# Attention and top-1 LoRA: projection products, scalings and one turned tile rearranged where one sequence follows another

## The chip, the cores and the metric

The kernel runs on one core of one Trainium2 chip. The metric is the device time of one launch in microseconds, as the median of several runs. Engines are named as in the profile: PE is TensorE, DVE VectorE, ACT ScalarE, POOL GpSimd, SP SyncE (which issues all DMAs here).

## The reference

Four sequences of 1024 rows and 1024 columns, all in fp32, pass through a pre-LayerNorm causal attention of 32 heads (32 columns each, rotary positions) and then through a LayerNorm and a top-1 choice among 8 LoRA adapters of rank 16. Cut to what is computed:

```
B, S, D, H, E, R = 4, 1024, 1024, 32, 8, 16
n = layernorm(x)
q, k, v = rotary(n @ wq), rotary(n @ wk), n @ wv       # per head of 32 columns
p = softmax(causal(q @ k.T / sqrt(32)))
y = x + (p @ v) @ wo
m = layernorm(y)
e, gate = argmax(m @ route_w.T), max(m @ route_w.T)    # per row, one of 8
out = y + gate * ((m @ A[e].T) @ Bw[e].T)
```

## The kernel before, in words

**Units.** The work is cut into 32 units (b, g): sequence b (0 to 3) and group g (0 to 7) of four heads, run in this order. A unit takes some 80 to 87 us. Unit 7 is the last of the first sequence, 15 of the second, 23 of the third, 31 of the fourth.

**The frame of a unit.** `SLOTS` gives eleven slots. Nine are score rounds (`score_round`, L393: small matmuls into the one PSUM buffer `s`, copied by ACT at L417, the mask added on POOL at L420); two, "second" and "first", multiply probabilities by values (`apply`: `av` at L573, into the same PSUM buffer; the sums' reciprocals `rec` at L534, their spread `by` at L547 and L548, the product `at` at L593). Behind each round DVE finds the rows' maxima (`top` L438, `both` L459), ACT takes the exponentials of an earlier round (L467), and DVE turns probabilities in blocks of 32 (L492) for `av`. Each engine works through its instructions in the order in which they are issued; what is issued late is behind everything issued before it.

**What fills a unit.** Between rounds, `fill` and `do_some` take steps from the list `between[u]`, a share after every round, by each step's cost (1.0 for one product). This list is written by hand for the changes of sequence and woven for the others. It holds:
- the chains of unit u+1 (`chain`, L302): q, k and v for either half of the rows, each 8 products of 128x512 (L313) into one PSUM bank; then ACT copies the bank out, and for q and k DVE and POOL apply the rotary (L345 to L351);
- `project` (L679) of the sequence before, for the row tile t = g: 16 products `po` (L690), two banks of 8; each takes a 256 KB piece of wo from one of four `chunk` buffers, and the load of the piece four places on is issued behind it. The second bank's end issues the residual sum (L696) and the LayerNorm of y (`find_moments`, and L186 into `yn`);
- the `tail` of the tile before, t = g-1, in four steps: `turn` (eight PE transposes into two PSUM banks `pt_f`, L198, copied out by ACT at L200 and by DVE at L204), `route` (16 products `ph`, L711, and a chain of five short DVE instructions to `wh`, L730), `turn_hidden` (one transpose `pw`, L740) and `adapt` (two matmuls `pf`, L750, two sums on DVE, L753, and the store of `out_y`, L754).

**The norm of the next sequence.** Class `Norm` (L233) prepares x of sequence b+1 tile by tile: `load`; `find` (two BATCH_NORM_STATS2 at L175, L177, L179 on DVE, then 1/sqrt on POOL, L181, as `rstd_a`); `scale` (L186 on DVE, in place); `turn` (eight transposes `pt_a`, L198, and two copies by ACT, L200 and L202, into `xnT`), which scales first if that hasn't been done, and then loads the tile named in `after`. Five rows of x stand in the pool `row`; at the later changes tiles 3, 4 and 6 are loaded into the buffers of `qT` and `kT` (`homes`). For b = 1, `scale` also finds the next tile's moments.

**Three changes of sequence.** Around units 5 to 7 (first), 15 (second) and 23 (third), the steps are written out by hand: `behind(last_v, at, step)` puts a step of the norm behind a given product of the list of the unit before, `between[-2].insert` into the list of the one before that, and `change_steps` (L788) builds the last unit's list. At the first change nothing else is there. At the second and third this list starts with eight products held back from unit 15's or 23's own chain v, second half (`h`), the tail of tile 6, and the projection of tile 7 (`p`); then come the new sequence's chains, with the rest of `p` woven in.

**PSUM.** Four banks in turn (`ps`: chains, `po`, `pt_a`, `pt_f`, `ph`, `pw`, `pf`, `pr`) and the buffer of four banks for `s` and `av`. A bank is taken again when its copy or sum is done.

Of the kernel before, what the change touches and what calls it, by code (L numbers as in the profile page):

```python
# [71 lines left out]
def tile_preln_attn_then_top1_lora(  # L72
# [26 lines left out]
    NT = S // P  # L99
# [91 lines left out]
    def transposed(dst, src, name, scalar_only=False):  # L191

        pts = []
        for half in range(NC // 4):
            pt = bank([P, 4, P], f"pt_{name}_{half}")
            for i in range(4):
                c = 4 * half + i
                nc.tensor.transpose(pt[:, i, :], src[:, c * P : (c + 1) * P], eye_sb)  # L198
            pts.append(pt)
        nc.scalar.copy(dst[:, 0:4, :], pts[0])  # L200
        if scalar_only:
            nc.scalar.copy(dst[:, 4:8, :], pts[1])  # L202
        else:
            nc.vector.tensor_copy(dst[:, 4:8, :], pts[1])  # L204
# [28 lines left out]
    class Norm:  # L233
# [24 lines left out]
        def find(self, t):  # L258
            while self.found <= t and self.found in self.x:
                k = self.found  # L260
                self.moments[k] = find_moments(self.x[k], f"a{self.b}_{k}")
                self.found += 1
# [24 lines left out]
        def scaling(self, t):  # L287
            return Step(lambda: self.scale(t), 0.0)

        def turning(self, t):  # L290
            return Step(lambda: self.turn(t), 2.0 if self.b == 0 else 1.3)
# [364 lines left out]
    def finish_steps(b, t, kind="stream"):  # L656
# [6 lines left out]
        st = {}  # L663
        name = f"{b}_{t}"
# [35 lines left out]

        def turn():
            st["ynT"] = st["yn"].rearrange("p (c k) -> p c k", k=P)
            transposed(st["ynT"], st["yn"], f"f{name}", scalar_only=at_end)

        def route(ks=None):
            ph = bank([P, E + ER], f"ph_{name}")
# [53 lines left out]
        chains = []  # L760
# [27 lines left out]
    def change_steps(u, norm, project, tail, held):  # L788

        p, h, turning, scaling = project, held, norm.turning, norm.scaling
        out, chains = [], []
        for n, tb in (("q", 0), ("k", 0), ("q", 1), ("k", 1), ("v", 0), ("v", 1)):
            chains += chain(u, n, tb)
        if p:
            turn, route, turn_hidden, adapt = tail
            find = norm.finding
            out += [*h[:2], turn, *h[2:4], turning(2), h[4], find(3), route, h[5], scaling(3), find(4)]
            out += [h[6], turn_hidden, h[7], p[0], adapt, Step(lambda: norm.load(7), 0.0), scaling(4)]  # L800
            out += [p[1], find(5), p[2], scaling(5), turning(3), p[3], p[4], turning(4), *p[5:8]]
            chains = weave(chains[:-6], p[8:]) + chains[-6:]
            out += [*chains[:2], find(6), *chains[2:4], scaling(6), turning(5), *chains[4:6], find(7)]
            out += [*chains[6:8], scaling(7), turning(6), *chains[8:14], turning(7)]
            return out + chains[14:]
        out += [*chains[:3], scaling(5), turning(4), *chains[3:7], scaling(6), turning(5)]
        out += [*chains[7:12], scaling(7), turning(6), *chains[12:16], turning(7)]
        return out + chains[16:]

    USUAL = (("q", 0), ("k", 0), ("q", 1), ("k", 1), ("v", 0), ("v", 1))  # L810
# [2 lines left out]
    def behind(steps, at, step):  # L813

        steps.insert(steps.index(at) + 1, step)
# [4 lines left out]
    for u, (b, g) in enumerate(units):  # L820
        project, new_tail = [], []
        if b:
            fetch, (project,), new_tail = finish_steps(
                b - 1, g, "resident" if u == len(units) - 1 else "stream"
            )
            if g:
                apart = 3 if g + 1 == NG and u + 1 < len(units) else 8
                between[-1].insert(max(0, len(between[-1]) - apart), fetch)
            else:
                late_fetch[u] = fetch  # L830

        if u + 1 < len(units) and g + 1 == NG:
            last_v = between[-1]
            if b:
                norm = Norm(b + 1, {0: (2,), 2: (5,), 3: (6,)}, {3: "q", 4: "k", 6: "q"})
                load = [Step(lambda norm=norm, t=t: norm.load(t), 0.0) for t in range(2)]
                for at, step in (
                    (own["k", 0][0], load[0]),  # L840
                    (own["v", 0][0], norm.finding(0)),
                    (own["v", 0][1], load[1]),
                    (own["v", 0][2], norm.scaling(0)),
                    (own["v", 0][6], norm.turning(0)),
                    (own["v", 0][7], norm.finding(1)),
                    (own["k", 1][0], norm.scaling(1)),
                    (own["k", 1][3], norm.turning(1)),
                    (own["k", 1][5], norm.finding(2)),
                    (own["k", 1][7], norm.scaling(2)),
                ):  # L850
                    behind(last_v, at, step)
            else:
                norm = Norm(b + 1, {0: (5,), 1: (6,), 2: (7,)})
                for t, at in enumerate((("k", 1), ("k", 1), ("k", 1), ("v", 1))):
                    behind(last_v, own[at][(1 + 3 * t) % NC], norm.turning(t))
                behind(last_v, own["v", 1][5], norm.scaling(4))
                behind(last_v, own["k", 0][0], norm.scaling(3))
                behind(last_v, own["q", 0][6], norm.scaling(2))
                for t in (1, 0):
                    between[-2].insert(18 + 22 * t, norm.scaling(t))  # L860
                between[-2].insert(0, Step(lambda norm=norm: norm.load(*range(TB + 1)), 0.0))
            steps = change_steps(u + 1, norm, project, tail, held)
            norms[b + 1] = norm
        else:
            steps = []
            held = []
            if u + 1 < len(units):


                ends = g + 2 == NG and b + 1 < B  # L870
                own = {}
                for n, tb in ENDING if ends else USUAL:
                    own[n, tb] = chain(u + 1, n, tb)
                    if ends and b and (n, tb) == ("v", 1):
                        held = own[n, tb]
                    else:
                        steps += own[n, tb]
            if not steps:
                steps = list(project)
            elif b and not g:  # L880
                steps = steps[:36] + weave(steps[36:], project)
            else:
                steps = weave(steps[:-6], project) + steps[-6:]
            if u + 1 == len(units):
                new_tail6 = tail
            n = len(steps)
            for k, s in reversed(list(enumerate(tail))):
                steps.insert(6 + k * n // 7, s)
        between.append(steps)
        tail = new_tail  # L890
# [248 lines left out]
```

## Time and profile before

| | |
|---|---|
| median of 3 runs | 2777.18 us (2774.65 to 2780.03) |
| profiled execution: time, span, mean granted PE clock | 2774.93 us, 2773.1 us, 0.994 |
| PE busy | 2695.8 us, 97% |
| DVE, ACT, POOL busy | 77%, 63%, 23% |
| DMA over the span | 113 GB/s |
| PE idle or waiting, second change (1170 to 1242 us) | 15.3 us |
| PE idle or waiting, third change (1857 to 1930 us) | 13.3 us |

How to read it: the span runs from the first to the last instruction on the core. The times of groups are read from one profiled execution. In a timeline row there stand the start in us, the duration, engine, line, operation, what is written and read, tile sizes and the number of instructions; in brackets the idle time ahead and the instruction that ended it. `pt_a`, `pt_f`, `st_a` and so on are tiles' names with the numbers left out. The granted clock is a share of full speed. A share of busy time over the whole span is a mean over many stages; the waits of an engine and the rows around them say which of them count.

### The profile page before, as it was taken

What the parts mean: (1) busy time and instruction counts of PE and PEld (TensorE: products, weight loads), DVE (VectorE), ACT (ScalarE), POOL (GpSimd) and SP (SyncE); (2) the same over time, 40 slices, a digit from 0 to 9 for tenths busy, and PEclk for the clock granted to TensorE, in tenths of its full rate; (3) what the DMA queues carried; (4) which work ended last, traced back from release to release, by engine and by line L of the source; (5) the groups of instructions that cost most, each with busy time, mean ns of one, the idle gap of its engine ahead of it and who ended that gap; (6) DMA issues with size and microseconds to landing.
All of it is one profiled execution on the core that took longest, in us unless ns stands there. A gap on an engine that the chain in (4) does not pass through costs nothing.

```text
span 2773.1 us, 84079 instructions
## 1 busy us (share of the span) xinstructions
PE 2695.8 (97%) x35328; PEld 1328.7 (48%) x35328; DVE 2133.2 (77%) x4201; ACT 1754.4 (63%) x5030; POOL 637.7 (23%) x900
## 2 busy tenths in 40 slices
PE   8999999899999999989999999998999999999998
PEld 5444444444444544445444455444544444544445
DVE  4888889887777777777777777887777777777655
ACT  2877787776666666656666666765566666666421
POOL 2222222222222222222222222212222222222000
PEclk9999999999999999999999999999999999999999
DMA  3222231225454445551644444454255444436421
GB/s 116 51 55 55 58 102 47 75 55 161 127 138 123 117 120 149 154 146 49 174 143 123 135 115 124 135 163 136 66 158 149 130 133 125 118 117 194 127 67 54
DMA packets 448011, 317.86 MB, mean 115 GB/s; under 512 B 150288, under 2 KB 371728, under 8 KB 447632
## 3 DMA queue, kind: packets, MB, share of 16 engines
q1 hardware_dynamic: 447632, 312.47, 40.4%
q8 instruction: 278, 4.55, 0.7%
q14 instruction: 101, 0.83, 0.1%
HBM read 262.59 MB, written 49.81 MB: 113 GB/s over the span
## 4 chain that ended last, share of the span: by engine, by line
PE 81%; DVE 14%; ACT 2%; POOL 1%; issue 1%; DMA 0%; SPq 0%; POOLq 0%; ACTq 0%; DVEq 0%
PE po L690 15%; PE pq L313 14%; PE pk L313 13%; PE pv L313 12%; PE s L406 11%; PE av L573 9%; DVE top L438 4%; DVE pr L492 4%; PE pf L750 2%; PE ph L711 2%; DVE both L459 1%; PE pr L547 1%; PE pt_f L198 1%; ACT pr L417 1%; ACT pr L467 1%
## 5 line engine op out<-in xcount | busy, mean ns | idle before, releaser
L467 ACT ACTIVATE pr<-pr,both 128x256 f32<-128x256 f32 (+15 forms) x2048 | 1045.0, 519 | 47.9 <-DVE both L459 47.5
L438 DVE TENSOR_REDUCE top<-pr 128x2 f32<-128x960 f32 (+15 forms) x768 | 651.1, 894 | 252.1 <-POOL pr L420 251.5
L417 ACT COPY pr<-s 128x640 f32<-128x640 f32 (+14 forms) x544 | 525.2, 1016 | 500.7 <-PE s L406 500.1
L492 DVE STREAM_TRANSPOSE pr<-pr 128x1024 f32<-128x1024 f32 (+11 forms) x768 | 664.4, 907 | 34.3 <-ACT pr L467 31.0
L313 PE MATMUL pv<-xnT,wv 128*128 128x512 f32 x1024 | 488.1, 604 | 0.0
L420 POOL TENSOR_TENSOR pr<-pr,causal_sb 128x128 f32<-128x128 f32 x512 | 238.7, 473 | 1077.1 <-ACT pr L417 1068.3
L313 PE MATMUL pq<-xnT,wq 128*128 128x512 f32 x1008 | 478.6, 601 | 0.6 <-ACT xnT L200 0.6
L313 PE MATMUL pk<-xnT,wk 128*128 128x512 f32 x1008 | 477.0, 603 | 2.0 <-ACT xnT L200 2.0
L406 PE MATMUL s<-kT,qT 32*32 32x256 f32 (+4 forms) x17408 | 394.3, 386 | 10.0 <-ACT pr L417 5.8
L467 ACT ACTIVATION_READ_ACCUMULATOR pr<-pr,both 128x1 f32 x2048 | 400.8, 196 | 0.0
L690 PE MATMUL po<-chunk,attn 128*128 128x512 f32 x736 | 377.3, 598 | 0.3 <-DMA chunk<-in_wo 0.3
L406 PEld LDWEIGHTS s<-kT,qT 32*32 32x32 f32 x17408 | 187.9, 103 | 268.0 <-issue 103.4
L313 PEld LDWEIGHTS pk<-xnT,wk 128*128 128x128 f32 x1008 | 182.2, 190 | 238.8 <-issue 234.9
L313 PEld LDWEIGHTS pv<-xnT,wv 128*128 128x128 f32 x1024 | 187.3, 192 | 217.7 <-issue 213.4
L313 PEld LDWEIGHTS pq<-xnT,wq 128*128 128x128 f32 x1008 | 182.1, 191 | 224.9 <-issue 221.2
L573 PE MATMUL av<-pr,vals 64*32 64x256 f32 (+3 forms) x12288 | 272.2, 319 | 6.6 <-DVE pr L492 5.8
L573 PEld LDWEIGHTS av<-pr,vals 64*32 64x32 f32 x12288 | 213.4, 106 | 114.3 <-issue 43.2
L459 DVE TENSOR_TENSOR both<-top 32x4 f32<-32x4 f32 (+3 forms) x1152 | 215.1, 187 | 23.8
L690 PEld LDWEIGHTS po<-chunk,attn 128*128 128x128 f32 x736 | 136.1, 191 | 164.5 <-issue 152.5
L548 ACT COPY by<-pr 128x512 f32<-128x512 f32 x64 | 37.5, 586 | 254.8 <-PE pr L547 254.8
L593 DVE TENSOR_TENSOR at<-av,by 128x256 f32<-128x256 f32 x128 | 48.1, 418 | 164.8 <-ACT by L548 164.8
L690 PE MATMUL po<-wo,attn 128*128 128x512 f32 x256 | 117.5, 600 | 0.0
(87 smaller groups left out, 1718.5 us busy)
## 6 DMA issues: line engine op xcount, KB each, us to landing
chunk<-in_wo SPq DMA_DIRECT2D x368, 256.0 KB, 3.5
vals<-vd SPq DMA_DIRECT2D x256, 128.0 KB, 4.1
x<-in_x SPq DMA_DIRECT2D x58, 512.0 KB, 5.7
wq<-in_wq SPq DMA_DIRECT2D x32, 512.0 KB, 4.0
wk<-in_wk SPq DMA_DIRECT2D x32, 512.0 KB, 3.9
wv<-in_wv SPq DMA_DIRECT2D x32, 512.0 KB, 4.3
vd<-vT SPq DMA_DIRECT2D x128, 128.0 KB, 4.8
out_y<-x SPq DMA_DIRECT2D x32, 512.0 KB, 2.8
```

Source lines behind the costliest of these rows:

```text
L313: nc.tensor.matmul(at["p"], lhsT=wt[:, c, :], rhs=xnTs[b, tb][:, c, :], start=(c == 0), stop=(c == NC - 1),)
L406: nc.tensor.matmul(sc[i * SQ : (i + 1) * SQ, h, at : at + w].rearrange("p (j k) -> p j k", k=SQ), lhsT=of_q[rows, 2 * t + half], rhs=of_k[ ...
L417: nc.scalar.copy(pr[:, :, k0 : k0 + w], sc[:, :, at : at + w])
L420: nc.gpsimd.tensor_tensor(diagonal, diagonal, causal_sb.unsqueeze(1).to_broadcast([P, HG, SQ]), ALU.add)
L438: nc.vector.tensor_reduce(top[:, k, h : h + step], places[u, t][:, h : h + step, :], AX.X, ALU.max, negate=True,)
L459: nc.vector.tensor_tensor(dst[rows], src[rows], src[other], op)
L467: nc.scalar.activation(pr[:, h, :], pr[:, h, :], AF.Exp, bias=tops[u, t][:, h : h + 1], accum_out=dens[u, t // QT][:, t % QT, h : h + 1],)
L492: nc.vector.transpose(pr, pr)
L573: nc.tensor.matmul(avs[half][h * HD : (h + 1) * HD, t0:, :], lhsT=v[rows, j, h * HD : (h + 1) * HD], rhs=rhs, start=(j == 0), stop=(j == n ...
L690: nc.tensor.matmul(st["po"], lhsT=lhsT, rhs=rhs, start=(c == start), stop=(c == stop))
L711: nc.tensor.matmul(ph, lhsT=st["ynT"][:, c, :], rhs=w[:, c - i * RA, :], start=(c == 0), stop=(c == NC - 1),)
L750: nc.tensor.matmul(pf, lhsT=st["whT"], rhs=rhs, start=True, stop=True)
```

## The change

Three things, all in the order in which steps are issued or in the engine that copies:

1. `turn` of a tail copies the second half by ACT (L202) instead of DVE (L204) for tile 6 (`t == NT - 2`) too. This is tile 6 of the first, second and third sequences, which runs at the second and third change and in unit 31; the fourth's is so already.
2. In `change_steps`, with a projection there: twelve products of `p` come ahead of the new chains, where there were eight (two changes, so eight products in all), four of them before `turn_hidden`, where there were none; finds and scalings have new places among them, and the turnings of tiles 2 and 3 are one to a few steps later. Without a projection (first change): `scaling(5)` leaves this list, `scaling(6)` and `scaling(7)` stand further ahead of their turnings.
3. Ahead of it: at the second and third change the finds of tiles 1 and 2 and the scaling of tiles 1 and 2 get earlier places in the list of unit 14 or 22. At the first change the scalings of tiles 0 and 1 go to earlier places in unit 5, those of tiles 2 to 5 in unit 6.

```diff
@@ -700,7 +700,8 @@
 
         def turn():
             st["ynT"] = st["yn"].rearrange("p (c k) -> p c k", k=P)
-            transposed(st["ynT"], st["yn"], f"f{name}", scalar_only=at_end)
+
+            transposed(st["ynT"], st["yn"], f"f{name}", scalar_only=at_end or t == NT - 2)
 
         def route(ks=None):
             ph = bank([P, E + ER], f"ph_{name}")
@@ -796,15 +797,16 @@
         if p:
             turn, route, turn_hidden, adapt = tail
             find = norm.finding
-            out += [*h[:2], turn, *h[2:4], turning(2), h[4], find(3), route, h[5], scaling(3), find(4)]
-            out += [h[6], turn_hidden, h[7], p[0], adapt, Step(lambda: norm.load(7), 0.0), scaling(4)]
-            out += [p[1], find(5), p[2], scaling(5), turning(3), p[3], p[4], turning(4), *p[5:8]]
-            chains = weave(chains[:-6], p[8:]) + chains[-6:]
+            load_last = Step(lambda: norm.load(7), 0.0)
+            out += [*h[:2], turn, *h[2:4], find(3), p[0], h[4], turning(2), h[5], p[1], route, scaling(3)]
+            out += [find(4), h[6], p[2], h[7], p[3], turn_hidden, scaling(4), *p[4:6], adapt, load_last]
+            out += [p[6], find(5), p[7], turning(3), scaling(5), *p[8:10], turning(4), *p[10:12]]
+            chains = weave(chains[:-6], p[12:]) + chains[-6:]
             out += [*chains[:2], find(6), *chains[2:4], scaling(6), turning(5), *chains[4:6], find(7)]
             out += [*chains[6:8], scaling(7), turning(6), *chains[8:14], turning(7)]
             return out + chains[14:]
-        out += [*chains[:3], scaling(5), turning(4), *chains[3:7], scaling(6), turning(5)]
-        out += [*chains[7:12], scaling(7), turning(6), *chains[12:16], turning(7)]
+        out += [*chains[:2], turning(4), scaling(6), *chains[2:6], turning(5), scaling(7)]
+        out += [*chains[6:11], turning(6), *chains[11:16], turning(7)]
         return out + chains[16:]
 
     USUAL = (("q", 0), ("k", 0), ("q", 1), ("k", 1), ("v", 0), ("v", 1))
@@ -841,23 +843,25 @@
                     (own["v", 0][0], norm.finding(0)),
                     (own["v", 0][1], load[1]),
                     (own["v", 0][2], norm.scaling(0)),
+                    (own["v", 0][4], norm.finding(1)),
                     (own["v", 0][6], norm.turning(0)),
-                    (own["v", 0][7], norm.finding(1)),
-                    (own["k", 1][0], norm.scaling(1)),
+                    (own["v", 0][7], norm.scaling(1)),
+                    (own["k", 1][2], norm.finding(2)),
                     (own["k", 1][3], norm.turning(1)),
-                    (own["k", 1][5], norm.finding(2)),
-                    (own["k", 1][7], norm.scaling(2)),
+                    (own["k", 1][5], norm.scaling(2)),
                 ):
                     behind(last_v, at, step)
             else:
                 norm = Norm(b + 1, {0: (5,), 1: (6,), 2: (7,)})
                 for t, at in enumerate((("k", 1), ("k", 1), ("k", 1), ("v", 1))):
                     behind(last_v, own[at][(1 + 3 * t) % NC], norm.turning(t))
-                behind(last_v, own["v", 1][5], norm.scaling(4))
-                behind(last_v, own["k", 0][0], norm.scaling(3))
-                behind(last_v, own["q", 0][6], norm.scaling(2))
+                behind(last_v, own["v", 1][6], norm.scaling(5))
+                behind(last_v, own["v", 1][3], norm.finding(5))
+                behind(last_v, own["k", 0][4], norm.scaling(4))
+                behind(last_v, own["q", 1][2], norm.scaling(3))
+                behind(last_v, own["q", 0][2], norm.scaling(2))
                 for t in (1, 0):
-                    between[-2].insert(18 + 22 * t, norm.scaling(t))
+                    between[-2].insert(10 + 16 * t, norm.scaling(t))
                 between[-2].insert(0, Step(lambda norm=norm: norm.load(*range(TB + 1)), 0.0))
             steps = change_steps(u + 1, norm, project, tail, held)
             norms[b + 1] = norm
```

The same products, transposes, scalings and loads are issued as before; three copies change their engine.

## The prediction

> **What bounds the kernel now.** I read the page first (busy shares, then the chain that ended last), then TensorE's waits, then the timeline around the places where TensorE waits, then windows of 5 and 20 us there.
>
> ```profile
> PE 2695.8 (97%) x35328; PEld 1328.7 (48%) x35328; DVE 2133.2 (77%) x4201; ACT 1754.4 (63%) x5030; POOL 637.7 (23%) x900
> PE 81%; DVE 14%; ACT 2%; POOL 1%; issue 1%; DMA 0%; SPq 0%; POOLq 0%; ACTq 0%; DVEq 0%
> ```
>
> PE is busy for 97% of the span and carries most of the chain. No matmul is removed or added, so the change can only win back PE's idle time, 77 us in all, and the time that PE runs at a lowered clock. The view of PE's waits says where that lies:
>
> ```profile
> PE pt_a L198 <- DVE x L186: 23.9, 8, 9.5
> PE ph L711 <- DVE yn L204: 9.3, 3, 3.6
> PE pw L740 <- DVE wh L730: 9.0, 2, 4.5
> ```
>
> (us in total, times, longest). The timeline of PE around the second change of sequence (units 15 to 16) places them; in brackets stands the idle time before a group and who ended it:
>
> ```profile
> 1174.66 1.10 PE L198 MATMUL pt_a<-eye_sb,x 128*128 128x128 f32 x8 [2.65 <-DVE x L186]
> 1175.59 3.60 PE L313 MATMUL pk<-xnT,wk 128*128 128x512 f32 x8
> ...
> 1188.27 1.06 PE L198 MATMUL pt_a<-eye_sb,x 128*128 128x128 f32 x8 [3.20 <-DVE x L186]
> ...
> 1195.40 2.80 PE L711 MATMUL ph<-chunk,yn 128*128 128x136 f32 x16 [3.63 <-DVE yn L204]
> 1197.99 2.93 PE L313 MATMUL pv<-xnT,wv 128*128 128x512 f32 x4
> 1205.41 0.45 PE L740 MATMUL pw<-eye_sb,wh 128*128 128x128 f32 x1 [4.49 <-DVE wh L730]
> ...
> 1240.18 1.98 PE L313 MATMUL pk<-xnT,wk 128*128 128x512 f32 x4 [1.00 <-ACT xnT L200]
> ```
>
> With waits of 0.2 to 0.3 us these come to 15.3 us idle. At the third change (23 to 24) the same five read 2.65, 1.51, 3.63, 4.49 and 1.00, 13.3 us. The windows show why (columns: PE, PEld, DVE, ACT, POOL busy with counts, granted clock, DMA):
>
> ```profile
> 1180.00:1200.00 20.00, 13.17 (x172) 8.29 (x157) 18.59 (x36) 11.80 (x32) 5.65 (x9) 0.92 0.41 139
> 1200.00:1220.00 20.00, 15.51 (x268) 8.50 (x268) 13.95 (x31) 5.10 (x18) 1.87 (x4) 0.83 0.51 158
> 1220.00:1240.00 20.00, 19.15 (x247) 9.66 (x234) 12.14 (x26) 11.81 (x37) 3.26 (x7) 1.00 0.69 171
> ```
>
> Up to 1207 DVE is full and PE starves; from 1210 PE is full and DVE has room. So PE work pulled ahead across that border pays, and so does DVE work taken out of the first stretch. The clock falls there too: 4 pv took 2.93 us at 1197.99, 1.88 at 1183.19. Such groups lose 2.6 us at the second change, and 3.2 at the third (its 8 pk at 1862.82 took 5.03, against 3.60 above).
>
> **The change, second and third boundary.** Eight products move (four per boundary, about 0.88 us each: 4 po take 1.98 with the first one's latency, 6 take 2.74), with the eight held pv and av's first half they now stand between the waiting transposes.
>
> DVE up to wh (1205.26 now): the L204 copy goes (0.69, pitch 0.73). find(1) right behind scale(0) removes the 1.09 us in which DVE waits at 1171.26 for POOL's L420, which stands behind rstd; find(2) behind yn removes the 0.73 before scale(2), and that scaling, 1.75 us beside POOL's L346 against 0.81 elsewhere, meets it no more (0.94). Sum 3.5, so wh ends about 1201.8.
>
> PE, followed instruction by instruction with the pitches of the rows above:
> - pt_a of tile 1: scale(1) now ends about 1170.9, s ends at 1172.0: the 2.65 goes.
> - pt_f at 1179.7, p0, then pt_a of tile 2. Its x is late no more, but it needs both PSUM banks of pt_f (pv, po and two pt_f hold the four). Both copies are now ACT's, behind three exps which wait for DVE's both at about 1184.5: PE arrives at 1184.1 and starts at 1186.8. **A new wait, 2.7**, behind which every matmul is queued. Between 1 and 4: it follows where ACT serves the second copy.
> - ph at about 1191.2 with both copies done: 3.63 goes. ACT pays two times 0.59 there, in a stretch where it is 59% busy.
> - p1 to p3, the last held pv and av's first half (3.7 us) are issued ahead of pw. PE arrives at 1201.4, pw starts about 1202: 4.49 becomes 0.6.
> - pt_a of tile 3: its second half needs the bank that ACT is copying from: 0.6 new. The next product waits 0.3 for DVE's L753.
> - On SP the chunks of the last early products and x of tile 6 queue behind out_y, whose store waits for the second L753 (about 1212.6). Chunks land in 3.3 us (median of the DMA view): 0 to 0.6, taken as 0.
> - pt_a of tile 6: scale(6) now stands behind top and both of row 15 on DVE. PE arrives at 1227.8, scale(6) ends about 1229.9: **a new wait, 2.1** (0 to 4); the tile ends at 1230.9 where it was 1238.15, with one pq and three products more done. The old 1.00 at pk goes with it.
>
> New waits: 2.7 + 0.6 + 0.6 + 0.3 + 2.1 = 6.3. Gain: 15.3 + 2.6 - 6.3 = 11.6 us, and 13.3 + 3.2 - 6.3 = 10.2 at the third boundary. Check by places: pt_a 6 ends 7.3 earlier with 4 x 0.88 = 3.5 more done, and 1.0 less wait follows: 11.8. Behind 1240 PE is busy 19.82 of 20 us with DVE waiting for it, so nothing is late next that would take this back.
>
> **The clock.** The Trainium skill ("TensorE: Matmul & The Clock Gate", section "What's actually happening") lets the clock halve after at least one idle window of about 3.4 us, and come back after about as long busy; by that the new waits of 2.7 and 2.1 cost no clock. The trace says otherwise:
>
> ```profile
> 1861.63 1.39 PE L198 MATMUL pt_a<-eye_sb,x 128*128 128x128 f32 x8 [2.65 <-DVE x L186]
> 1862.82 5.03 PE L313 MATMUL pk<-xnT,wk 128*128 128x512 f32 x8
> ```
>
> A wait of 2.65 cost 1.43 us here and nothing at 1174.66; 3.20 at 1188.27 and 1.51 cost nothing. One in four: for the four new long waits I take 4 x 1.43 / 4 = 1.4 us (rule 0, worst 5.7).
>
> **Unit 31** runs tile 6 of the third sequence too, so its L204 goes as well:
>
> ```profile
> 2561.76 1.97 PE L711 MATMUL ph<-chunk,yn 128*128 128x136 f32 x8 [2.00 <-DVE yn L204]
> ```
>
> ACT's first copy starts at 2557.93; a second behind it ends about 2559.0, before PE has done the first eight ph (2559.75). Gain 2.0. The exps behind it come 0.5 us later, into ACT's idle 6.66 us. If that cover were gone: 0.5.
>
> **First boundary (units 5 to 7).** No products move here; scalings and finds go to earlier places, in a stretch where DVE is full too.
>
> ```profile
> 539.32 1.09 PE L198 MATMUL pt_a<-eye_sb,x 128*128 128x128 f32 x8 [2.95 <-DVE x L186]
> ...
> 546.34 1.09 PE L198 MATMUL pt_a<-eye_sb,x 128*128 128x128 f32 x8 [0.72 <-DVE x L186]
> 550.33 5.91 PE L573 MATMUL av<-pr,vals 64*32 64x256 f32 x128 [2.90 <-DVE pr L492]
> ```
>
> av of unit 7 waits for DVE's L492, which has scale(4), find(5), scale(5) and find(6) ahead of it. Now scale(6) and find(7) come ahead as well: scale 0.73 + find 1.63 = 2.4 more (the rstd wait of 0.67 may add). The 2.95 and 0.72 go, and av's wait takes them up: about 9.4 us in one piece, av 2.4 later with the same seven pq done. In unit 5 find(0), scale(0) and find(1), 4.7 us, go ahead of DVE's at, which had 2.8 idle: s is 0.7 late; scale(1) and find(2) ahead of another: 1.2 late, at the s that waits 3.44 (446.71). In unit 6 POOL's L420 no longer stands behind rstd, which gives back what is asked there: 0. Sum **-4.2** (-7 to -2). The clock: av already takes 5.91, 3.68 at 399.75, so 2.2 are paid now; a longer wait adds 0, up to 2.
>
> **The sum.** 11.6 + 10.2 + 2.0 - 4.2 - 1.4 = 18.2 us. From the profiled execution (2774.9, span 2773.1) that is 2756.7; from the median of the runs, 2777.2, it is **2759.0**, -0.66%. A measurement of this kernel can tell about 0.2%, 5.6 us, from no change.
>
> **The rivals.**
> - *The waits only change their names* (0.14). DVE is the bound up to 1207, and products that PE does early only make it wait elsewhere: only DVE's own savings count, 3.5 + 3.5 + 2.0 - 4.2 = 4.8, so 2772.4. For it: DVE 18.59 of 20. Against: PE is full from 1210 on, so early products must shorten that stretch.
> - *Every wait at the two boundaries goes* (0.10): ACT serves pt_f at once and scale(6) is in time. 17.9 + 16.5 + 2.0 = 36.4, less 4.2: 2745. Against: the copies' place behind the exps in ACT's row.
> - *Slower, by one transfer* (0.05). The load of x's tile 6 is issued on SP behind out_y's store, beside the chunks. By my walk it is issued at 1212.6 and, at 5.7 us (page, x<-in_x), lands at 1218.3; find(6) wants it at 1220.7. Late, it stops DVE in its order, ahead of top and both, so the exps and pt_a of tile 6: each us past 2.4 of slack costs one, at both boundaries. From 18.2 / 2 = 9.1 us past it (landing after 1230) this decides; at 13 past it the time is 2785. For it: DMA is 69% busy from 1220 to 1240. Against: qT's loads take 4.0 there now.
> - *Scaling is no farther from its turn where it matters*: true at tile 6 and at the first boundary, and part of the sum.
>
> **How the numbers follow.** The forecast's case has 0.71. Its own range, from the open ends (pt_a 2, pt_a 6, the clock, the first boundary), is 2750 to 2769. To leave out no more than 2 in 10 the range goes to 2746 to 2773, which takes in the first rival. Faster: 0.69 of the forecast's case, 0.03 of the first rival and 0.10 of the second, 0.82; same 0.12 (0.02 and 0.10); slower 0.06 (0.01 and the transfer).
>
> **What would show it.** The waits of ph for L204 and of pw for L730 are gone or under 1 us; pt_a of tile 2 waits for ACT's copy of yn (2 to 3), pt_a of tile 6 for x's L186 (about 2) ahead of tile 6's turn; ph in unit 31 has no wait for DVE; near 543 to 553 one long wait of av for L492. Wrong if the two boundaries are shortened by under 7 us each, if av's wait at the first one costs nothing, or if a find of tile 6 waits for its load.

## The result, and the profile after

The change takes 2752.48 us (median of 6 runs, 2747.70 to 2754.03) where the kernel before takes 2776.47 (6 runs): the ratio is 0.9911, with a 95% interval of 0.9901 to 0.9922. That is 24 us, where 18.2 were forecast (2759.0, in a range from 2746 to 2773). The profiled execution of the change is the shortest of the six, 2747.7 us with a span of 2745.9, so its 27.2 us against the profile of before overstate the gain a little.

To see where the time went, match a group of matmuls that both kernels have and compare its start. I use the four transposes of L547, which every unit has twice. These two rows are the same group, the first of unit 16's two, from the timeline of PE before and then after:

```profile
1313.48 0.66 PE L547 MATMUL pr<-eye_sb,by 128*128 128x128 f32 x4
```

```profile
1300.46 0.66 PE L547 MATMUL pr<-eye_sb,by 128*128 128x128 f32 x4
```

Here the change is 13.02 us ahead. The difference between two such leads is what a stretch has won. All tables below are made in this way, against the profile of before:

| us won in | first boundary (units 5 to 7) | second | third | unit 31 |
|---|---|---|---|---|
| forecast, clock not yet taken off | -4.2 | 11.6 | 10.2 | 2.0 |
| the change | 2.3 | 11.3 | 10.3 | 4.0 |
| the change, profiled a second time | 2.7 | 8.3 | 10.1 | 4.0 |

In these two profiles the leads stay within 0.7 us everywhere else from the first boundary on. PE's waits after the change, as the view of waits lists them (us in total, times, longest):

```profile
PE av L573 <- DVE pr L492: 11.6, 2, 9.1
PE pt_a L198 <- DVE x L186: 9.8, 2, 9.1
...
PE pt_a L198 <- ACT yn L200: 5.2, 2, 2.6
PE pt_a L198 <- DVE qT L186: 4.5, 2, 2.3
PE po L690 <- DMA chunk<-in_wo: 4.0, 5, 1.7
...
PE pw L741 <- DVE wh L731: 0.9, 2, 0.5
```

The 9.3 us of ph for L204 are gone and the 9.0 of pw for wh are 0.9. Of the 23.9 us of pt_a for L186, 9.8 are left; 9.1 of them are one wait in the first unit, which the change doesn't touch. What has come instead: pt_a for ScalarE's copy of yn and pt_a for tile 6's scaling (in a buffer of qT) are new rows; av for L492 was 5.8 in three waits, and products that wait for their chunk of wo were 0.3. The timeline of PE at the second boundary has them in place:

```profile
1184.96 1.14 PE L198 MATMUL pt_a<-eye_sb,x 128*128 128x128 f32 x8 [2.60 <-ACT yn L200]
...
1189.43 2.02 PE L712 MATMUL ph<-chunk,yn 128*128 128x136 f32 x16
...
1199.45 0.33 PE L741 MATMUL pw<-eye_sb,wh 128*128 128x128 f32 x1 [0.47 <-DVE wh L731]
...
1208.91 0.66 PE L198 MATMUL pt_a<-eye_sb,qT 128*128 128x128 f32 x4 [0.68 <-ACT xnT L200]
...
1215.73 1.98 PE L690 MATMUL po<-chunk,attn 128*128 128x512 f32 x4 [1.57 <-DMA chunk<-in_wo]
...
1228.94 1.06 PE L198 MATMUL pt_a<-eye_sb,qT 128*128 128x128 f32 x8 [2.26 <-DVE qT L186]
```

Five waits, of which four were forecast nearly at their size (2.7, 0.6, 0.6, 2.1). The fifth, 1.57 for a chunk, was put at 0 to 0.6 and taken as 0. Nothing else in the stretch waits: pk after tile 6, 1.00 before, doesn't.

### The profile page after: what moved, and what is told of

The parts are those of the page before. It is cut to its first block, busy times and chain, and to the rows that moved or that the text cites. A ratio compares the mean times of both kernels' runs of the same rounds, so it can differ in the third digit from the quotient of the medians.

```text
span 2745.9 us, 84082 instructions
## 1 busy us (share of the span) xinstructions
PE 2682.2 (98%) x35328; PEld 1322.0 (48%) x35328; DVE 2126.7 (77%) x4198; ACT 1755.0 (64%) x5033; POOL 638.1 (23%) x900
## 4 chain that ended last, share of the span: by engine, by line
PE 80%; DVE 14%; ACT 2%; DMA 1%; POOL 1%; issue 1%; SPq 0%; POOLq 0%; DVEq 0%; ACTq 0%
PE po L690 14%; PE pq L313 14%; PE pk L313 13%; PE pv L313 12%; PE s L406 11%; PE av L573 9%; DVE top L438 4%; DVE pr L492 4%; PE ph L712 2%; PE pf L751 2%; DMA chunk<-in_wo 1%; DVE both L459 1%; PE pr L547 1%; ACT pr L417 1%; PE pt_f L198 1%
## 5 line engine op out<-in xcount | busy, mean ns | idle before, releaser
L417 ACT COPY pr<-s 128x640 f32<-128x640 f32 (+14 forms) x544 | 525.3, 1017 | 492.3 <-PE s L406 491.7
L492 DVE STREAM_TRANSPOSE pr<-pr 128x1024 f32<-128x1024 f32 (+11 forms) x768 | 664.3, 907 | 33.3 <-ACT pr L467 30.1
L406 PE MATMUL s<-kT,qT 32*32 32x256 f32 (+4 forms) x17408 | 393.0, 385 | 10.7 <-ACT pr L417 7.2
L573 PE MATMUL av<-pr,vals 64*32 64x256 f32 (+3 forms) x12288 | 273.2, 320 | 11.7 <-DVE pr L492 11.6
L459 DVE TENSOR_TENSOR both<-top 32x4 f32<-32x4 f32 (+3 forms) x1152 | 213.4, 185 | 23.7
```

The costliest lines, as they stand in the source:

```text
L406: nc.tensor.matmul(sc[i * SQ : (i + 1) * SQ, h, at : at + w].rearrange("p (j k) -> p j k", k=SQ), lhsT=of_q[rows, 2 * t + half], rhs=of_k[ ...
L417: nc.scalar.copy(pr[:, :, k0 : k0 + w], sc[:, :, at : at + w])
L459: nc.vector.tensor_tensor(dst[rows], src[rows], src[other], op)
L492: nc.vector.transpose(pr, pr)
L573: nc.tensor.matmul(avs[half][h * HD : (h + 1) * HD, t0:, :], lhsT=v[rows, j, h * HD : (h + 1) * HD], rhs=rhs, start=(j == 0), stop=(j == n ...
```

## The experiments

Each was run beside the kernel before on one chip, not always the same one, so runs are best compared by their ratios to it; the 95% interval is in brackets. The last columns are us won by stretch in the run's profile. In the profile of finds_only the first boundary, which it doesn't touch, reads 1.8, so differences of 2 us in one cell of one profile are not told apart from chance. change_again is the change run once more: unit 5's wait for at is 1.37 us there again (1.4 expected), and av of unit 7 waits 7.73 (9 expected).

| run | median us | ratio | first | second | third | unit 31 |
|---|---|---|---|---|---|---|
| change_again | 2750.83 | 0.9907 [0.9893, 0.9920] | 2.7 | 8.3 | 10.1 | 4.0 |
| first_old | 2752.42 | 0.9907 [0.9892, 0.9922] | -0.7 | 8.8 | 6.7 | 4.0 |
| first_only | 2774.72 | 0.9990 [0.9982, 0.9999] | 3.0 | 0.8 | -0.5 | 0.1 |
| act_only | 2771.08 | 0.9978 [0.9968, 0.9988] | -0.1 | 0.9 | 0.1 | 3.9 |
| order_only | 2776.29 | 0.9999 [0.9991, 1.0008] | -0.2 | 0.0 | -0.4 | 0.2 |
| finds_only | 2769.24 | 0.9975 [0.9965, 0.9985] | 1.8 | 3.9 | 2.6 | 0.3 |
| order_act | 2760.22 | 0.9938 [0.9925, 0.9950] | -0.5 | 8.2 | 6.8 | 4.0 |
| eight_ahead | 2744.00 | 0.9877 [0.9864, 0.9891] | 3.3 | 14.1 | 12.1 | 4.0 |
| scale6_early | 2751.28 | 0.9911 [0.9897, 0.9924] | 1.6 | 10.7 | 9.1 | 4.0 |
| turn2_late | 2757.92 | 0.9928 [0.9916, 0.9941] | 2.9 | 7.5 | 5.2 | 4.0 |
| best1 | 2747.35 | 0.9894 [0.9881, 0.9908] | 3.4 | 11.1 | 10.1 | 3.4 |
| best2 | 2736.41 | 0.9858 [0.9843, 0.9873] | 5.0 | 15.7 | 14.7 | 4.0 |

### The first boundary: first_old and first_only

first_old is the change with these lines of before:

```diff
-        out += [*chains[:2], turning(4), scaling(6), *chains[2:6], turning(5), scaling(7)]
-        out += [*chains[6:11], turning(6), *chains[11:16], turning(7)]
+        out += [*chains[:3], scaling(5), turning(4), *chains[3:7], scaling(6), turning(5)]
+        out += [*chains[7:12], scaling(7), turning(6), *chains[12:16], turning(7)]
...
-                    between[-2].insert(10 + 16 * t, norm.scaling(t))
+                    between[-2].insert(18 + 22 * t, norm.scaling(t))
```

first_only is before with the opposite edit (the five `behind` lines of this boundary go with it in both).

> The change with its first boundary (units 5 to 7) put back as it was before; the second and third boundary and the copies by ScalarE stay. Forecast's theory: the first boundary costs 4.2 us in the change, so this runs at about 2748 (ratio 0.990) and is faster than the change. Rival, from the one trace of the change: unit 7 lost 2.4 there but units 5 and 6 won 4.6 (a wait of 3.44 for the product at, and the lowered clock behind it, are gone), so this is slower than the change by some 2 us, about 2755 (ratio 0.992). In the trace both want av of unit 7 to wait 2.9 again instead of 9.05; they differ in the time from unit 5 to unit 6.

> Before, with the change's first boundary (units 5 to 7) alone. Forecast: 4.2 us slower, about 2781.5. Rival, from the trace of the change: 2.3 us faster, about 2775, with two parts that show in the profile: the matmul groups around unit 5's and 6's waits are some 4.6 us earlier (wait for at 3.4 to 1.4, and no lowered clock behind it), and av of unit 7 waits 9 us in one piece, 2.4 more than the three waits of before.

first_old measured the same as the change, and its intervals allow 4 us either way, so it decides nothing by its time; its trace, from unit 5 to unit 6 (the table below), is back at the time of before, as the rival has it. first_only is 2.8 us faster than before (0.3 to 5 by its interval): the forecast's loss of 4.2 is excluded. The timeline of PE around unit 5's wait, before and then first_only:

```profile
446.71 2.42 PE L406 MATMUL s<-kT,qT 32*32 32x384 f32 x64 [3.44 <-DVE at L593]
449.06 4.57 PE L313 MATMUL pv<-xnT,wv 128*128 128x512 f32 x6
```

```profile
444.40 1.51 PE L406 MATMUL s<-kT,qT 32*32 32x384 f32 x64 [1.08 <-DVE at L593]
445.84 2.84 PE L313 MATMUL pv<-xnT,wv 128*128 128x512 f32 x6
...
455.45 1.44 PE L406 MATMUL s<-kT,qT 32*32 32x256 f32 x64 [1.72 <-ACT pr L417]
```

The wait for at falls from 3.44 to 1.08, though a scaling and a find more stand ahead of it. The lowered clock behind it goes too: s and pv take 4.35 instead of 6.99. But the clock is not what the unit gains by. act_only, which has the old order here, shows the same wait with full clock behind it:

```profile
447.40 1.49 PE L406 MATMUL s<-kT,qT 32*32 32x384 f32 x64 [3.45 <-DVE at L593]
448.82 2.84 PE L313 MATMUL pv<-xnT,wv 128*128 128x512 f32 x6
```

Its unit 5 is no shorter for it: what the matmuls saved is waited again behind them (1.75 for ACT's copy of s, 1.13 for L492). The time from one group of L547 to the next, in the profiles with the old order (before, first_old, act_only, order_only, finds_only, order_act) and with the change's (the change twice, first_only, eight_ahead, scale6_early, turn2_late):

| us | old order, six profiles | change's order, six profiles | loss forecast |
|---|---|---|---|
| within unit 5 | 31.6 | 32.2 | 0.7 |
| unit 5 to unit 6 | 41.8 | 37.8 to 38.1 | 1.2 |
| within unit 6 | 34.0 to 34.1 | 32.8 to 32.9 | 0 |
| unit 6 to unit 7 | 43.6 to 45.9 | 46.3 to 46.9 | 2.4 |

From unit 5 to unit 6 the old order took 41.8 us in all six, though the matmuls' own time in it goes from 38.1 down to 35.5. So DVE sets the time there, and the gain has to be looked for in its row. Its chain as far as the sums' reciprocals (rec, L534), which the next L547 needs, before and then first_only:

```profile
445.84 0.72 DVE L593 TENSOR_TENSOR at<-av,by 128x256 f32<-128x256 f32 x2
456.76 1.81 DVE L438 TENSOR_REDUCE top<-pr 128x2 f32<-128x768 f32 x2 [1.08 <-POOL pr L420]
473.15 0.76 DVE L534 TENSOR_TENSOR rec<-den 32x16 f32<-32x16 f32 x4
```

```profile
443.54 0.71 DVE L593 TENSOR_TENSOR at<-av,by 128x256 f32<-128x256 f32 x2
450.93 1.81 DVE L438 TENSOR_REDUCE top<-pr 128x2 f32<-128x768 f32 x2
469.20 0.71 DVE L534 TENSOR_TENSOR rec<-den 32x16 f32<-32x16 f32 x4
```

Counted from L547, at comes 2.4 us earlier. From at to rec DVE takes 25.7 instead of 27.3: the wait of 1.08 for POOL is gone, and two L459 take 0.67 instead of 0.93 and 0.97. Together that is the 4.0 us by which first_only's next L547 is ahead. Why at is earlier, windows from 405 to 447 us say; the third busy value is DVE's. Before, then first_only:

```profile
405.00:447.00 42.00, 38.36 (x595) 18.04 (x607) 32.73 (x68) 30.21 (x90) 13.75 (x18) 0.99 0.31 71
```

```profile
405.00:447.00 42.00, 40.05 (x645) 18.97 (x644) 36.94 (x75) 31.26 (x91) 15.03 (x19) 1.00 0.34 77
```

DVE does 4.2 us more in the same 42. It had been idle there in front of an earlier at (2.78 us), in front of maxima that wait for POOL (1.56, 1.70) and elsewhere; the earlier finds and scalings run in this idle time, and the place that they left (420 to 425 us) is free for the work ahead of the next at. In unit 7 the forecast's loss is there. From the change's profile:

```profile
548.09 5.90 PE L573 MATMUL av<-pr,vals 64*32 64x256 f32 x128 [9.05 <-DVE pr L492]
```

One wait of 9.05 where 9.4 was forecast, and the stretch around it, from unit 6's L547 to unit 7's, loses 1.0 to 1.6 us against before in the profiles that have this part.

### One part of the later boundaries at a time: act_only, order_only, finds_only, order_act

act_only is before with one line of the change, order_only with its list and nothing else, order_act with both:

```diff
-            transposed(st["ynT"], st["yn"], f"f{name}", scalar_only=at_end)
+            transposed(st["ynT"], st["yn"], f"f{name}", scalar_only=at_end or t == NT - 2)
```

```diff
+            out += [*h[:2], turn, *h[2:4], find(3), p[0], h[4], turning(2), h[5], p[1], route, scaling(3)]
+            out += [find(4), h[6], p[2], h[7], p[3], turn_hidden, scaling(4), *p[4:6], adapt, load_last]
...
```

finds_only is before with the finds and scalings of tiles 1 and 2 in the change's places (`behind`, b > 0).

> Before, with tile 6 of sequences 0 to 2 copied out by ScalarE alone and nothing else. Theory 1 (DVE's own chain up to wh sets the second and third boundary): ph loses its wait of 3.63 at both, but pw waits longer for wh, about 7.4 instead of 4.49, since DVE is relieved of 0.73 only; 0.7 us per boundary and 2.0 in unit 31, 3.5 us in all, about 2773. Rival (each wait that goes counts): 2 x 3.6 + 2.0 = 9 us, about 2767.

> Before, with the change's list for the last unit of the second and third sequence (products ahead, finds and scalings among them) and nothing else; the finds and scalings of tiles 1 and 2 and the copies stay as before. Theory 1: wh comes no earlier than before (the waits for scale 1, scale 2 and L204 stay), but four products, the last held pv and half of av stand ahead of pw; some 6.8 us per boundary after the new waits behind pw, 13.6 us in all, about 2763. Rival (the gain is that DVE is relieved and scalings come in time): under 5 us, about 2772.

> Before, with the earlier finds and scalings of tiles 1 and 2 at the second and third boundary and nothing else. Theory 1 (up to wh DVE's chain is the bound, so what is taken out of it counts): the waits at pt_a of tiles 1 and 2 (2.65 and 3.20, 1.51) go, DVE loses 1.09 + 0.73 + 0.94 = 2.8 us per boundary ahead of wh; the rest comes back as longer waits at ph and pw: 2 x 2.8 = 5.5 us, about 2771. Rival (the removed waits all count): 2.65 + 3.20 + 2.65 + 1.51 = 10 us and the clock, about 2766. Second rival (all of it comes back at pw, as with the list alone): 2776 to 2777.

> Before, with the change's list for the last unit (as in order_only) and its copies by ScalarE (as in act_only), without the moved finds and scalings of the units before and without the first boundary. Theory 1 (the list needs the copy: in order_only pt_a of tile 2 waited 6.15 us for L204 to free its bank): that wait falls to about 2.6, the wait for scale 1 (2.65) stays, and 6 to 8 us per boundary are won besides unit 31's 4: about 2760. Rival (the parts add up: 0 for the list, 6 for the copies): about 2771.

act_only: at the second boundary ph no longer waits, and pw waits for both. From its timeline of PE:

```profile
1192.71 2.12 PE L711 MATMUL ph<-chunk,yn 128*128 128x136 f32 x16
...
1205.70 0.44 PE L740 MATMUL pw<-eye_sb,wh 128*128 128x128 f32 x1 [9.15 <-DVE wh L730]
```

The 3.63 at ph is gone, the 3.20 at tile 2 is 1.52, and the 4.49 at pw has become 9.15 (about 7.4 was expected). wh can't come before DVE has done what is queued ahead of it, so a wait ahead of ph that goes is waited again at pw; the stretch won 0.9 at the second boundary and 0.1 at the third. Most of act_only's 6 us is unit 31's 3.9. The same holds for finds_only. There pt_a of tile 1 doesn't wait; the two rows are tile 2's and pw:

```profile
1182.72 0.88 PE L198 MATMUL pt_a<-eye_sb,x 128*128 128x128 f32 x4 [2.84 <-DVE x L186]
...
1199.59 0.44 PE L740 MATMUL pw<-eye_sb,wh 128*128 128x128 f32 x1 [6.17 <-DVE wh L730]
```

ph waits 1.26 instead of 3.63, and pw 6.17 instead of 4.49. What remains are 3.9 and 2.6 us, about what was to leave DVE's chain (2.8 by the forecast), and not the waits that went.

order_only refutes what I expected of it: 0 instead of 13.6 us. Its timeline of PE has one wait that I had not followed into it:

```profile
1188.40 0.60 PE L198 MATMUL pt_a<-eye_sb,x 128*128 128x128 f32 x4
1195.15 1.11 PE L198 MATMUL pt_a<-eye_sb,x 128*128 128x128 f32 x4 [6.15 <-DVE yn L204]
```

The second half of pt_a of tile 2 needs pt_f's second PSUM bank. With L204 that bank is free only when DVE reaches the copy, at the end of what is queued ahead of it, and behind pt_a stand all products that the list has put ahead. In order_act, with the copy on ScalarE, pt_a of tile 2 doesn't wait at all, where 2.6 was expected (PE comes there late enough, since the wait for scale 1 stays). List and copy together bring 8.2 and 6.8 us, where the copy alone brought 0.9 and 0.1: theory 1, with 2760.22 us against 2760 expected. By their ratios list and copy come to 0 + 6.1 us alone and to 17 together, so some 11 us are the two needing each other. With the 6.9 of finds_only and the 2.8 of first_only that is 27, a little more than the change's 25.

### How many products ahead: eight_ahead and scale6_early

Both start from the change:

```diff
-            out += [p[6], find(5), p[7], turning(3), scaling(5), *p[8:10], turning(4), *p[10:12]]
-            chains = weave(chains[:-6], p[12:]) + chains[-6:]
+            out += [p[6], find(5), p[7], turning(3), scaling(5), turning(4)]
+            chains = weave(chains[:-6], p[8:]) + chains[-6:]
```

```diff
-            out += [*chains[:2], find(6), *chains[2:4], scaling(6), turning(5), *chains[4:6], find(7)]
+            out += [*chains[:2], find(6), chains[2], scaling(6), chains[3], turning(5), *chains[4:6], find(7)]
```

> The change with eight products ahead of the new chains, as before, instead of twelve: p8 to p11 are woven into the chains again; the order up to p7 stays. Theory 1 (only what stands ahead of pw fills a gap): nothing is lost, and the wait of 1.6 us for a chunk between p11 and p10 goes, while the wait for scale 6 stays at about 2; 0 to 3 us faster than the change, 2750 to 2752. Rival (each product ahead counts 0.88): 8 x 0.88 = 7 us slower than the change, about 2759.5.

> The change with the scaling of tile 6 one product earlier, which puts it ahead of row 15's maxima on DVE. Theory 1 (eight_ahead is faster because its shorter list puts this scaling ahead of row 15, and because no four products in a row wait for chunks): the wait of 2.26 at pt_a of tile 6 goes at both boundaries, the chunk's 1.6 stays; 4.5 us faster than the change, about 2747. Rival (the wait only moves to the next copy or product): 2751 to 2752.

Without the eight more products the kernel is faster than with them: 2744.0 (2742.0 to 2746.3) against 2750.83 and 2752.48, 7 to 9 us by medians and ratios, and more than I expected. Two waits are gone or shorter, which makes 6.2 us of the difference between this profile and the change's first (1.57 and 1.53 at the second boundary, 1.73 and 1.35 at the third). The first is the chunk's. Behind pw the change has p8 to p11 with little between them. A chunk is loaded when the product four places ahead is done, and lands some 3.3 us after its issue (median of the view of transfers around the second boundary of before); four products are done in 3.5. The second profile of the change shows that this is on the edge:

```profile
1215.57 1.12 PE L690 MATMUL po<-chunk,attn 128*128 128x512 f32 x2 [1.40 <-DMA chunk<-in_wo]
1218.01 2.07 PE L690 MATMUL po<-chunk,attn 128*128 128x512 f32 x2 [1.32 <-DMA chunk<-in_wo]
1219.88 4.35 PE L313 MATMUL pq<-xnT,wq 128*128 128x512 f32 x8
```

Two waits, 2.7 us, and behind them the clock lowered: po took 2.07 and pq 4.35, against 1.12 and 3.60 beside. That is most of the 3.1 us by which the second boundary differs between the two profiles of one kernel. The second wait is tile 6's scaling, whose place on DVE follows from where the list is cut by the score rounds. From DVE's timeline, the change and then eight_ahead:

```profile
1224.84 2.35 DVE L438 TENSOR_REDUCE top<-pr 128x2 f32<-128x1024 f32 x2 [4.14 <-POOL pr L420]
...
1227.98 0.81 DVE L186 TENSOR_SCALAR qT<-qT,mv_a,rstd_a 128x1024 f32<-128x1024 f32 x1
```

```profile
1219.84 0.81 DVE L186 TENSOR_SCALAR qT<-qT,mv_a,rstd_a 128x1024 f32<-128x1024 f32 x1 [0.73 <-POOL rstd_a L181]
...
1223.43 2.35 DVE L438 TENSOR_REDUCE top<-pr 128x2 f32<-128x1024 f32 x2 [0.53 <-POOL pr L420]
```

In the change DVE sits idle for 4.14 us and has the scaling ready behind the maxima of row 15. In eight_ahead the scaling is ahead of them, and PE waits 0.73 for it instead of 2.26.

scale6_early does the second without the first, and my expectation failed: the wait of 2.26 went, and the time didn't move. Its timeline of PE:

```profile
1217.08 1.12 PE L690 MATMUL po<-chunk,attn 128*128 128x512 f32 x2 [1.66 <-DMA chunk<-in_wo]
1219.18 1.13 PE L690 MATMUL po<-chunk,attn 128*128 128x512 f32 x2 [0.98 <-DMA chunk<-in_wo]
...
1229.11 1.04 PE L198 MATMUL pt_a<-eye_sb,qT 128*128 128x128 f32 x8
1230.79 1.13 PE L313 MATMUL pk<-xnT,wk 128*128 128x512 f32 x2 [0.64 <-ACT rawq L339]
```

0.64 came back at pk, and the chunks cost 6.3 us in all in this profile (4.0 and 5.5 in the two of the change). The clock took its part too: against the change's first profile the waits between the groups of L547 are 0.9 and 1.7 us shorter at the two boundaries, and the matmuls themselves 1.4 and 2.8 us longer (granted clock 0.96 from 1870 to 1915 us, 1.00 from 1868 to 1913 in the change). So the two causes are there, but how the 7 to 9 us divide between them is not settled: the chunks' part changes from one execution to the next, and no run has the chunks mended alone.

### The new wait at tile 2: turn2_late, best1 and best2

turn2_late is the change with one step moved:

```diff
-            out += [*h[:2], turn, *h[2:4], find(3), p[0], h[4], turning(2), h[5], p[1], route, scaling(3)]
+            out += [*h[:2], turn, *h[2:4], find(3), p[0], h[4], h[5], p[1], turning(2), route, scaling(3)]
```

best1 and best2 combine what had been seen; `free(s)` is a step with cost 0, so that the cut by the score rounds falls elsewhere. best2, its core:

```diff
+            out += [*h[:2], turn, *h[2:4], find(3), p[0], free(h[4]), free(p[1]), free(h[5]), turning(2), route]
+            out += [scaling(3), find(4), h[6], p[2], h[7], *p[3:6], turn_hidden, scaling(4), *p[6:8]]
+            out += [adapt, load_last, p[8], find(5), p[9], turning(3), scaling(5), turning(4)]
+            chains = weave(chains[:-6], p[10:]) + chains[-6:]
+            out += [*chains[:2], find(6), chains[2], scaling(6), chains[3], turning(5), *chains[4:6], find(7)]
...
+        out += [*chains[:2], turning(4), *chains[2:6], turning(5), *chains[6:8], scaling(6)]
+        out += [*chains[8:11], scaling(7), turning(6), *chains[11:16], turning(7)]
```

In best1 the first line has `p[0], h[4], h[5], p[1], turning(2), route`, as in turn2_late, and h6, p2 and h7 have cost 0.

> The change with the turning of tile 2 two products later (behind p1 instead of behind h4), by when ScalarE has copied pt_f out. Theory 1 (up to pw DVE's chain sets the time): the wait of 2.6 us at pt_a of tile 2 goes, and the same time is waited at av's first half (for L492) and at pw (for wh); within 1 us of the change, about 2752. Rival (each wait that goes counts): 2 x 2.6 = 5.2 us faster than the change, about 2747.

> A version made from what the runs show: the turning of tile 2 behind p1; two more products ahead of av's first half and of pw, two fewer behind pw (ten in all ahead of the chains, none of them four in a row behind pw); scaling of tile 6 ahead of row 15's maxima; in the first sequence the scalings of tiles 6 and 7 behind av's first half. Theory 1: 2 x 1.8 us more than the version with eight ahead (2744), since two products fill the wait of 2.5 at pt_a of tile 2, and 2.4 at the first boundary: about 2738. If filling does nothing there (a bank or a chunk takes the time): 2742 to 2744.

> A second version from what the runs show. As best1, but the turning of tile 2 keeps its place ahead of the next score round, so that its copies stand ahead of that round's on ScalarE; p1 and a held product go ahead of it, into the wait of 2.5 for the copies of pt_f, and p3 and p4 ahead of av's first half; scaling of tile 6 ahead of row 15's maxima; the first sequence's scalings of tiles 6 and 7 behind av's first half. Theory 1: 2 x 1.8 us less than eight_ahead at the two boundaries and 0.8 to 2 at the first: ratio about 0.986, 2739. Rival (ScalarE is the bound there as in turn2_late): ratio 0.9877 or more, 2744 to 2747.

turn2_late was neither of the two: it is 5 to 7 us slower than the change. Its timeline of PE, then of ScalarE:

```profile
1190.41 3.51 PE L712 MATMUL ph<-chunk,yn 128*128 128x136 f32 x16 [4.37 <-ACT xnT L200]
```

```profile
1186.01 1.85 ACT L417 COPY pr<-s 128x768 f32<-128x768 f32 x3
...
1189.78 0.58 ACT L200 COPY xnT<-pt_a 128x512 f32<-128x512 f32 x1
```

With two products between, the turning falls behind the next score round. ph needs a bank that pt_a of tile 2 holds, and the copy that frees it now stands on ScalarE behind the copies of s (L417) and the exponentials after them. The wait of 2.6 became one of 4.4 further on, with ph at a lowered clock (3.51 against 2.02). best1 has the same step and the same fault, 5.08 us there. It gained back part of it by the rest: 2747.35 us, where 2738 was expected, and not faster than eight_ahead.

best2 keeps the turning ahead of the score round and puts p1 and one held product into the wait. Its timeline of PE:

```profile
1180.07 1.14 PE L198 MATMUL pt_a<-eye_sb,x 128*128 128x128 f32 x8 [0.87 <-ACT yn L200]
...
1182.71 2.12 PE L712 MATMUL ph<-chunk,yn 128*128 128x136 f32 x16
...
1194.57 0.33 PE L741 MATMUL pw<-eye_sb,wh 128*128 128x128 f32 x1 [0.37 <-DVE wh L731]
...
1217.43 1.06 PE L198 MATMUL pt_a<-eye_sb,qT 128*128 128x128 f32 x8 [0.75 <-DVE qT L186]
```

2.60 is 0.87, 2.26 is 0.75, pw still waits under half a microsecond, and chunks cost 0.2 us in the whole kernel. At the first boundary av of unit 7 waits 6.8 us instead of 9.05. The result is 2736.41 us, ratio 0.9858 where 0.986 was expected: 39 us faster than before, and 14 to 16 faster than the change.

## Why the prediction was right, and where it was not

- **What bounds.** DVE's chain up to wh set the time up to pw, and PE set it behind. act_only and finds_only show it: removed waits came back at pw, and what remained was about what DVE no longer had to do.
- **The walk through the second and third boundary** came out at its number in part by luck. Between the groups of L547 around a boundary both kernels run the same matmuls, so the gain there divides into waits of PE that went and matmuls that ran faster:

| us won | second: forecast | change | again | third: forecast | change | again |
|---|---|---|---|---|---|---|
| waits of PE | 9.0 | 7.4 | 6.3 | 7.0 | 5.6 | 5.4 |
| the matmuls' own time | 2.6 | 3.9 | 2.0 | 3.2 | 4.7 | 4.7 |
| sum | 11.6 | 11.3 | 8.3 | 10.2 | 10.3 | 10.1 |

- **Waits.** Four of the new ones were right to 0.2 us, and the 0.3 for L753 (now L754) was not there. **The mis-sized term is the chunks of wo, "0 to 0.6, taken as 0"**: they cost 1.6 to 2.7 us per boundary. I had followed SP's queue behind out_y, and not that products four in a row are used up about as fast as a chunk lands.
- **The matmuls' own time.** The lowered clock of before had cost more than the 2.6 and 3.2 of the walk. Right behind pw stand two groups that it does not name; at full clock each takes 1.02 us:

```profile
1205.65 1.92 PE L313 MATMUL pv<-xnT,wv 128*128 128x512 f32 x2
1207.35 1.91 PE L690 MATMUL po<-chunk,attn 128*128 128x512 f32 x2
```

- **That the list depends on the copy** was in the walk (the banks of pt_f), but costed as a wait of 2.7. order_only shows that with L204 it would have been 6.15, and the list worth nothing.
- **The eight more products.** I wrote that work pulled across the border pays. For those ahead of pw it does (order_act, eight_ahead). For p8 to p11, which stand behind pw where PE is full anyway, it doesn't, and their place brought the two waits that eight_ahead is without or has shorter.
- **The clock.** 1.4 us were taken off for the four new long waits: in the first profile none cost anything, in the second the chunks' waits did. By the rule weighed there (the Trainium skill, "TensorE: Matmul & The Clock Gate", section "What's actually happening": about 3.4 us idle) none of these would have cost anything. The runs have waits below 3.4 us of both kinds, and in act_only one of 3.45 with full clock behind it, so it decides nothing here.
- **Unit 31, 2.0 forecast, 3.4 to 4.0 measured** in the runs with the copy. The wait of 2.00 went as forecast. The missing term is the lowered clock behind it: before, the last eight ph took 1.97 us and the six po behind them 3.69; after, both are at full speed:

```profile
2563.52 3.69 PE L690 MATMUL po<-wo,attn 128*128 128x512 f32 x6
```

```profile
2535.38 2.12 PE L712 MATMUL ph<-chunk,yn 128*128 128x136 f32 x16 [0.79 <-ACT yn L200]
2537.34 2.74 PE L690 MATMUL po<-wo,attn 128*128 128x512 f32 x6
```

- **The first boundary, -4.2 forecast, +2.3 and +2.7 measured: the wrong step.** Unit 7's part had its sign (-2.4 forecast, -1.0 to -1.6 measured), and so had the first at of unit 5 (-0.7 forecast, -0.6 measured). The second at of unit 5 was counted by what goes ahead of it, without what leaves the place behind it: DVE's idle time took the earlier steps in, and where I had a loss of 1.2 the change won 3.7. In unit 6, put at 0, two small waits (0.35 and 0.60) went, and 1.3 was won.
- **The sum.** From 18.2, the first boundary gives 6.5 and 6.9 in the two profiles, unit 31 gives 2.0, the two later boundaries with the clock's 1.4 give 1.2 and -2.0, and the rest of the kernel -0.8 and -1.5: 27.1 and 23.6, where the medians differ by 24. So the total is nearer than its parts: the first boundary, forecast as a loss, makes most of the difference.
- **The rivals.** That only DVE's savings count is what act_only and finds_only show, where no product is ahead; with the list it is not so. The late load of tile 6's x, named as a sign of being wrong, came: find(6) waited for it 0.29 us in the change's first profile, 1.18 and 1.48 in its second, and up to 1.45 in eight_ahead. It stayed within the slack: PE waits 2.26 us for scale(6) at both boundaries in both profiles of the change. That every wait goes came closest in best2, with 15.7 and 14.7 of 17.9 and 16.5.

## What to carry to other kernels

Where two engines bound a stretch one after the other, a wait that is removed on the second pays only if the first engine's chain gets shorter or other work is put ahead of the next meeting point; here, work put ahead behind that point paid nothing and outran its loads. The same holds for the clock: a faster matmul shortens nothing where it only reaches the next wait sooner. With few PSUM banks the place of a copy in its engine's queue decides when the matmuls go on, so a new order of matmuls has to be walked through that queue too, and past the points where the list is cut. When steps are moved, count what their old place is now free for, not only what they delay in the new one. And a sum that comes out right is to be checked by its terms: here two of them were off in opposite directions.

## What the runs showed of the hardware that was not expected

- TensorE's clock was lowered around waits of 2 us and less: around the 2.00 of unit 31 in before (granted clock 0.91 from 2550 to 2570 us, 1.00 from 2530 to 2550 after) ph and the next six po took 1.9 us more than after. Waits of 2.60 and 2.26 in the change's first profile cost nothing; around the two chunk waits of 1.40 and 1.32 in the second (0.91 from 1205 to 1225 us, 1.00 in the first) two po and eight pq took 1.7 us more.
- What follows one and the same wait differs from execution to execution: behind unit 5's 3.44 the six pv took 4.57, 4.56, 4.49, 3.72, 3.21 and 2.84 us in the six profiles with the old order, and the stretch took 41.8 us in all of them.
- One kernel's boundary differs by 3 us from one execution to the next, by the landing of chunks that are on the edge and the clock that follows. Single profiles of such a stretch are not told apart below that.
